# Pacing table lookups by shares of a tile, with all gates transposed on TensorE, in a fused attention and lookup-FFN block

## The chip, the cores and the metric

The kernel runs on one core of a Trainium2 chip, in float32. A core has five engines with instruction queues of their own: TensorE (PE in the profile; its weight loads are PEld), VectorE (DVE), ScalarE (ACT), GpSimd (POOL) and SyncE (SP, which here only issues transfers). Each engine works through its queue strictly in order, and waits for the others by semaphores. Transfers are issued from SP's, ScalarE's or GpSimd's queue and run on 16 DMA engines. The metric is the device time of one execution in microseconds.

## What is computed

Input x has 8 sequences of 1024 tokens of 512 features. Per sequence:

```python
xn = layernorm(x)
q = xn @ Wq; gate = softmax(xn @ Wg)            # three gates for each token
for i in range(3):
    k, v = xn @ Wk[i], xn @ Wv[i]
    w = sigmoid(decay[i]) ** max(t - s - 1, 0) * (s after t)
    blended += gate[..., i:i+1] * (((q @ k.T) * w) @ v)
s = blended @ Wo * out_scale
W = lut[idx]                                     # 16 values; gate, up and down matrices, 1376 x 512 each
h = silu(xn @ Wgate.T) * (xn @ Wup.T)
out = x + s * silu(h @ Wdown.T)
```

## The kernel before, in words

There are two phases. Phase 1, to about 597 us, does the normalization, the projections, the attention recurrence and the building of the lookup weights, and writes its results to DRAM. Phase 2 does the two FFN products from there, with a seven-product scheme whose sums are made beforehand. The diff touches phase 1 alone.

Phase 1 is written as coroutines (Python generators) that one loop interleaves; every `yield` ends a portion of work. After tracing, `keep_order` fixes each engine's order to the order in which the instructions were written. So what decides when an instruction gets its turn is where its coroutine was resumed.

The loop of `phase_1` runs over sequences b (one more round than there are sequences) and in each over 8 steps k. A step resumes, in three thirds:

- `newer`, `project` of sequence b. It loads 128-token chunks of x, makes their statistics, normalizes them, transposes them on TensorE (`pt`, copied by ScalarE to `xnT`), and multiplies with the value and gate weights (`values`, tile `pv`). From step 4 on it also runs `features` for half 1 of the tokens, which makes queries and keys by seven products out of sums `t1` to `t4` (tile `ts`; `t1` on L505) that VectorE makes, and `softmax`, which makes the gates.
- `ending`, the last part of `project` of sequence b-1: `features` and `softmax` for half 0. It runs in steps 0 to 3.
- `older`, `chunks` of sequence b-1: the recurrence over chunks c = 7 to 0. TensorE transposes the keys (`pk`), makes scores (`psc`), adds to the state (`pu`) and makes the output (`po`, first with the factor `qb`, then with `pr`). VectorE makes `pr` out of `psc` (L652), and `ga`, the gated queries of the next chunk (L627); GpSimd makes `qb` out of `ga` (L631). ScalarE copies `po` to `bl` (L675), which is one buffer for all sequences and goes to DRAM at the end of each (L689).
- `weights`, the building of the lookup weights, through `build_some`, three times in a step.

The lookup of a tile (`look_up`, 128 partitions x 1024 indices; some tiles are narrower) is 19 VectorE instructions: three mask bits (L218), one on the index's lowest bit (L221), eight leaves (L225), seven selections (L242). Then GpSimd makes sums of the tile: four of 256 elements a partition (L272 to L276, or L322 to L326), and after every second tile four of 896 elements (L290 to L300, or L339 to L346). A looked-up tile lies in one of two `wgu` buffers. SP loads the indices of a tile while the tile before it is looked up.

`build_some(n)` resumes the building n times. The counts in the loop are 1, 0 and 0 or 1, 1 and 2 for b = 0, and for b = 1 to 7 they go (1, 1, 4), (1, 2, 5), (1, 2, 4), (1, 2, 3). A sum on GpSimd counts as one resumption like an instruction on VectorE, and some resumptions do nothing (three behind a pair of tiles, eight behind a pair of the down matrix).

The gates of half a sequence (`g`, 128 tokens x 12) must lie in DRAM as 12 rows of 128, so that they can be loaded into all partitions (`ga`, L473). `write` stores g's 1536 words one by one from SP's queue (L458). For (b, half) = (0, 1) alone, `turn` transposes g on TensorE (`pg`, L463), lets ScalarE copy it (`gs`, L465) and stores 12 rows from ScalarE's queue (L466). `pg` takes one of the three rotating PSUM buffers of tag `c`, which `pt`, `pv`, `pk`, `psc` and `po` share. `defer(n, ...)` holds an issue back for n calls of `tick()`, of which a step has three; the load of `ga` is deferred by 6.

Of the kernel before, what the change touches and what calls it, by code (L numbers as in the profile page):

```python
# [9 lines left out]
F32 = mybir.dt.float32  # L10
# [4 lines left out]
ALU = mybir.AluOpType  # L15
AX = mybir.AxisListType

P = 128
# [30 lines left out]
def recurrent_block(ctx: ExitStack, tc, x, wq, wk, wv, wo, wg, decay_logits, out_scale, lut, gidx, uidx, didx, out):  # L49
# [52 lines left out]
    bl_d = [dram.tile([P, T], F32, name=f"bld{b}", tag=f"bld{b}") for b in range(B)]  # L102
# [31 lines left out]
    def defer(parts, issue):  # L134
        later.append([parts, issue])
# [77 lines left out]
    def look_up(build, dst, iv, rows, n):  # L213

        bits = [build.tile([P, n], U8, name=f"bit{j}", tag=f"bit{j}") for j in (1, 2, 3)]
        low = iv.bitcast(U8).rearrange("p (n four) -> p n four", four=4)[:, :, 0]
        for j in (1, 2, 3):
            nc.vector.tensor_scalar(bits[j - 1][:rows, :n], low, 1 << j, None, ALU.bitwise_and)  # L218
            yield

        nc.vector.tensor_scalar(iv, iv, 31, 31, ALU.logical_shift_left, ALU.arith_shift_right)  # L221
        yield

        def leaf(o, k):
            nc.vector.tensor_scalar(  # L225
                o.bitcast(I32),
                iv,
                lut_x[:rows, k, :],
                lut_i[:rows, k, 0:1],
                ALU.bitwise_and,  # L230
                ALU.bitwise_xor,
            )

        def tree(o, level, k):
            if level == 0:
                leaf(o, k)
                yield
                return
            t = build.tile([P, n], F32, name=f"leaf{level}", tag=f"leaf{level}")
            yield from tree(o, level - 1, k)  # L240
            yield from tree(t[:rows, :n], level - 1, k + (1 << (level - 1)))
            nc.vector.copy_predicated(o, bits[level - 1][:rows, :n], t[:rows, :n])  # L242
            yield

        yield from tree(dst, 3, 0)

    def ffn_weights(build, pool, pair_pool):
# [8 lines left out]
        upper = []  # L256

        def gate_up(o):
            s, m = OCH[o]
# [42 lines left out]
            for _ in range(3):  # L302
                yield

        def down_tail():
            s, m = OCH[-1]
            idx = build.tile([P, NB], I32, name="idx", tag="idx", bufs=2)
            nc.sync.dma_start(out=idx[:m, :V], in_=didx[s : s + m, :])
            yield
            wf = pool.tile([P, 2 * NB], F32, name="wgu", tag="wgu", bufs=2)  # L310
            yield from look_up(build, wf[:m, :V], idx[:m, :V], m, V)
            defer(2, lambda: nc.sync.dma_start(out=wdt_d, in_=wf[:m, :V]))

        def down(rows, e, ends):
            idx = build.tile([P, NB], I32, name="idx", tag="idx", bufs=2)
            for a, row in enumerate(rows):
                nc.sync.dma_start(out=idx[:, ts(a, V)], in_=didx[ts(row, P), :])
            yield
            t = pool.tile([P, 2 * NB], F32, name="wgu", tag="wgu", bufs=2)
# [3 lines left out]
            nc.gpsimd.tensor_tensor(t2, b22, t1, ALU.subtract)  # L323
            yield
            nc.gpsimd.tensor_tensor(b12, b22, b12, ALU.subtract)
# [13 lines left out]
            nc.gpsimd.tensor_tensor(pair[:, :, 0], b12, b11, ALU.subtract)  # L339
            yield  # L340
            nc.gpsimd.tensor_tensor(b12, b22, b12, ALU.subtract)
            defer(2, lambda: nc.sync.dma_start(out=to[:, :, 0:2, :], in_=up))
            yield
            nc.gpsimd.tensor_tensor(pair[:, :, 1], b22, pair[:, :, 0], ALU.subtract)
            yield
            nc.gpsimd.tensor_tensor(pair[:, :, 2], b21, pair[:, :, 1], ALU.subtract)  # L346
            defer(4, lambda: nc.sync.dma_start(out=to[:, :, 4:7, :], in_=pair))
            for _ in range(8):
                yield
# [4 lines left out]
        yield  # L354
        for job, following in zip(jobs, jobs[1:] + [iter(())]):
# [21 lines left out]
    def project(b, pools, sides, kept):  # L377
# [61 lines left out]
        def softmax(hf):  # L439
# [15 lines left out]

            def write():
                with nc.allow_non_contiguous_dma(reason="1536 words"):
                    nc.sync.dma_start(out=there.rearrange("k p -> p k"), in_=g.rearrange("p c i -> p (c i)"))  # L458

            def turn():  # L460

                pg = p_c.tile([n * NI, P], F32, name=f"pg{b}_{hf}", tag="c")
                nc.tensor.transpose(pg, g.rearrange("p c i -> p (c i)"), ident)  # L463
# [9 lines left out]
            defer(6, lambda: nc.sync.dma_start(out=ga, in_=there.partition_broadcast(P)))  # L473

        def features(hf):
# [4 lines left out]

            qk[hf] = att.tile([P, NI + 1, U], F32, name=f"qk{b}_{hf}", tag=f"qk{hf}", bufs=1)
            c11, c12, c21, c22 = (qk[hf][:, 2 * j : 2 * j + 2, ts(c, H)] for j in (0, 1) for c in (0, 1))
            ts_ = tp.tile([P, 4, 2, H], F32, name=f"ts{b}_{hf}", tag=f"ts{hf}")
            b11, b12, b21, b22 = (xnT[:, 2 * v : 2 * v + 2, ts(2 * hf + c, H)] for v in (0, 1) for c in (0, 1))
            t1, t2, t3, t4 = (ts_[:, k] for k in range(4))
            a11, a12, s3, a22 = (wqk_sb[:, 2 * v : 2 * v + 2, ts(j, 2 * D)] for j in (0, 1) for v in (0, 1))
            s1, s2, s4 = (wqs[:, k] for k in range(3))
# [16 lines left out]
            there = xs_d[b][:, :, ts(hf, H)]  # L504
            nc.vector.tensor_tensor(t1, b12, b11, ALU.subtract)  # L505
            yield
            product(pa, 1, True)
# [55 lines left out]
        for k in range(NC):  # L563
# [25 lines left out]
            if k >= NC // 2:  # L589
                next(of_half, None)  # L590
            yield
        of_half = features(0)
        for k in range(NC // 2):
            yield
            if k == 0:
                next(of_half)
            next(of_half)
            half = softmax(0) if k == 0 else iter(())
            next(half, None)
            yield  # L600
            next(half, None)
            next(of_half, None)
            yield
# [10 lines left out]
    def chunks(b, pools, kept):  # L614
# [20 lines left out]
        for c in reversed(range(NC)):  # L635
# [52 lines left out]
            yield  # L688
        (nc.scalar if at_end else nc.sync).dma_start(out=bl_d[b], in_=bl)  # L689

    def phase_1():
        nonlocal small, p_a, p_c, p_r
        with (
# [21 lines left out]

            def build_some(n):
                for _ in range(n):
                    next(weights, None)

# [11 lines left out]
            for b in range(B + 1):  # L731
                following = project(b + 1, pools, sides, kept) if b + 1 < B else iter(())
                older = chunks(b - 1, (chk, blp), kept) if b else iter(())
                for k in range(NC):


                    if b == 0:
                        steps = (k > 0, k >= NC // 2, 2 * (k >= NC // 2))
                    elif b < B:
                        steps = ((1, 1, 4), (1, 2, 5), (1, 2, 4), (1, 2, 3))[k % 4]  # L740
                    else:
                        steps = (1, 0, 0)
                    tick()
# [12 lines left out]
                    next(newer, None)  # L756
                    build_some(steps[1])
                    next(older, None)
                    build_some(steps[2])
                    if k < NC // 2:  # L760
# [680 lines left out]
```

## Time and profile before

| | |
|---|---|
| three runs | 2112.64, 2113.19, 2113.54 us (median 2113.19) |
| the profiled execution | 2114.02 us, of which the span of the instructions is 2111.9 |
| granted TensorE clock, mean | 0.999 |
| 0 to 600 us: PE, DVE, ACT, POOL busy | 582.8, 511.2, 374.2, 302.0 us |
| 600 to 2111 us: PE, DVE, ACT, POOL busy | 1505.8, 933.0, 569.5, 738.4 us |
| lookups on VectorE (L218, L221, L225, L242) | 51, 17, 136 and 119 instructions |
| `gTd<-g`, the stores of gates by words | 15, of 6 KB, 14.7 us from issue to landing |
| `bld<-bl` | 7 from SP's queue, of 512 KB, 3.0 us |

In the profile an engine's idle time is put down to what ended it. The end of a matmul is modelled, so that a shown wait of TensorE is somewhat shorter than what the distance between two starts tells. A float32 matmul of the program shows as two in the profile, a transpose as one.

### The profile page before, as it was taken

What the parts mean: (1) busy time and instruction counts of PE and PEld (TensorE: products, weight loads), DVE (VectorE), ACT (ScalarE), POOL (GpSimd) and SP (SyncE); (2) the same over time, 40 slices, a digit from 0 to 9 for tenths busy, and PEclk for the clock granted to TensorE, in tenths of its full rate; (3) what the DMA queues carried; (4) which work ended last, traced back from release to release, by engine and by line L of the source; (5) the groups of instructions that cost most, each with busy time, mean ns of one, the idle gap of its engine ahead of it and who ended that gap; (6) DMA issues with size and microseconds to landing.
All of it is one profiled execution on the core that took longest, in us unless ns stands there. A gap on an engine that the chain in (4) does not pass through costs nothing.

```text
span 2111.9 us, 32189 instructions
## 1 busy us (share of the span) xinstructions
PE 2088.6 (99%) x11691; PEld 1752.9 (83%) x11691; DVE 1444.2 (68%) x2214; ACT 943.6 (45%) x2116; POOL 1040.4 (49%) x1050
## 2 busy tenths in 40 slices
PE   9999999999999999999999999999999999999999
PEld 7877878888878888887878888887978888797877
DVE  8889897889735675575567556656755665675567
ACT  4766666676434424423441442344144324423531
POOL 4554564364445447516543751655275255527432
PEclk9999999999999999999999999999999999999999
DMA  8765779657864744464454446345544634464442
GB/s 217 146 180 165 188 176 199 161 153 138 157 204 150 256 155 159 162 223 142 157 196 174 157 147 245 136 155 173 197 160 151 248 123 153 160 223 147 150 155 108
DMA packets 184635, 361.51 MB, mean 171 GB/s; under 512 B 50927, under 2 KB 122238, under 8 KB 184478
## 3 DMA queue, kind: packets, MB, share of 16 engines
q1 hardware_dynamic: 169894, 335.20, 52.7%
q0 software_dynamic: 4480, 14.68, 1.7%
q10 hardware_dynamic: 10104, 9.58, 1.5%
q8 instruction: 93, 1.52, 0.3%
q14 instruction: 64, 0.52, 0.1%
HBM read 282.87 MB, written 76.55 MB: 170 GB/s over the span
## 4 chain that ended last, share of the span: by engine, by line
PE 76%; DVE 3%; DMA 1%; issue 0%; ACT 0%; SPq 0%; DVEq 0%; ACTq 0%
PE s L885 33%; PE sE L885 6%; PE s12d L1139 5%; PE s21d L1139 5%; PE s11d L1139 5%; PE fs L833 3%; PE pd L1252 3%; PE ps L1259 3%; PE sEd L1139 2%; PE fsE L833 1%; PE pv L434 1%; PE s11d L1150 1%; PE s21d L1150 1%; PE s12d L1150 1%; PE sEd L1150 1%; PE po L674 1%
## 5 line engine op out<-in xcount | busy, mean ns | idle before, releaser
L885 PE MATMUL s<-xs,wq 128*128 128x256 f32 x3264 | 731.2, 379 | 0.0
L885 PEld LDWEIGHTS s<-xs,wq 128*128 128x128 f32 x3264 | 619.5, 190 | 95.9 <-issue 8.4
L908 DVE TENSOR_TENSOR s<-s,e 128x512 f32<-128x512 f32 x136 | 95.1, 699 | 204.4 <-ACT s L907 204.3
L1223 POOL TENSOR_TENSOR cu<-cu 128x256 f32<-128x256 f32 x32 | 35.1, 1097 | 306.4 <-DVE cl L1222 306.4
L434 PE MATMUL pv<-wvg_sb,xnT 128*128 128x387 f32 x512 | 177.6, 488 | 0.0
L816 POOL TENSOR_TENSOR xs<-xs 128x256 f32<-128x256 f32 x224 | 170.9, 789 | 8.1 <-PE fs L833 3.5
L912 DVE TENSOR_TENSOR sE<-s,e 128x512 f32<-128x512 f32 x136 | 95.0, 698 | 104.6 <-PE s L885 104.6
L976 POOL TENSOR_TENSOR u<-u,e 128x512 f32<-128x512 f32 x64 | 79.9, 1270 | 148.8 <-DVE u L972 130.3
L903 ACT COPY e<-sE 128x512 f32<-128x512 f32 x136 | 79.6, 585 | 138.8 <-PE sE L885 138.5
L885 PE MATMUL sE<-xs,wq 128*128 128x256 f32 x544 | 139.6, 379 | 0.0
L434 PEld LDWEIGHTS pv<-wvg_sb,xnT 128*128 128x128 f32 x512 | 94.4, 191 | 53.9
L980 POOL TENSOR_TENSOR h<-h,u 128x512 f32<-128x512 f32 x64 | 80.1, 1272 | 112.9 <-DVE u L987 100.3
L896 ACT COPY s<-s 128x512 f32<-128x512 f32 x136 | 77.5, 570 | 109.0 <-PE s L885 106.7
L413 POOL TENSOR_SCALAR rstd<-rstd 128x1 f32<-128x1 f32 x56 | 28.8, 515 | 192.3 <-ACT junk L412 186.4
L907 ACT COPY s<-s 128x512 f32<-128x512 f32 x136 | 77.5, 570 | 98.1 <-PE s L885 98.1
L1139 PE MATMUL s12d<-wdd,z 128*128 128x128 f32 x896 | 118.5, 275 | 0.6 <-ACT s12d L1161 0.6
L885 PEld LDWEIGHTS sE<-xs,wq 128*128 128x128 f32 x544 | 103.4, 190 | 14.1
L1139 PEld LDWEIGHTS s12d<-wdd,z 128*128 128x128 f32 x896 | 109.0, 192 | 0.8 <-ACT s12d L1161 0.8
L631 POOL TENSOR_TENSOR qb<-ga,q_tab 128x384 f32<-128x384 f32 x56 | 79.0, 1410 | 55.0 <-DVE ga L627 49.0
L225 DVE TENSOR_SCALAR leaf<-idx,lut_x,lut_sb 128x1024 int32<-128x1024 int32 (+2 forms) x119 | 96.5, 832 | 0.0
L242 DVE COPY_PREDICATED leaf<-bit,leaf 128x1024 f32<-128x1024 uint8 (+2 forms) x68 | 94.2, 1385 | 1.5
L1263 POOL TENSOR_TENSOR gx<-gx,cu 128x512 f32<-128x512 f32 x32 | 40.7, 1277 | 82.0 <-DVE cu L1261 64.5
(263 smaller groups left out, 4534.2 us busy)
## 6 DMA issues: line engine op xcount, KB each, us to landing
wq<-quadd SPq DMA_DIRECT2D x112, 896.0 KB, 4.5
wdd<-wdd SPq DMA_DIRECT2D x56, 896.0 KB, 4.6
xs<-xsd SPq DMA_DIRECT2D x56, 512.0 KB, 6.1
wq<-quadd SPq DMA_DIRECT2D x48, 448.0 KB, 4.1
x<-in_x SPq DMA_DIRECT2D x64, 256.0 KB, 4.7
xsd<-ts SPq DMA_DIRECT2D x16, 1024.0 KB, 14.9
gx<-in_x SPq DMA_DIRECT2D x64, 256.0 KB, 5.3
out<-gx POOLq DMA_DIRECT2D x56, 256.0 KB, 2.3
```

What stands on the lines that cost most here:

```text
L225: nc.vector.tensor_scalar(o.bitcast(I32), iv, lut_x[:rows, k, :], lut_i[:rows, k, 0:1], ALU.bitwise_and, ALU.bitwise_xor,)
L242: nc.vector.copy_predicated(o, bits[level - 1][:rows, :n], t[:rows, :n])
L434: nc.tensor.matmul(pv, lhsT=xnT[:, v, ts(c, P)], rhs=wvg_sb[:, v, :], start=(v == 0), stop=(v == NV - 1))
L816: nc.gpsimd.tensor_tensor(o, x1, x2, ALU.subtract)
L833: nc.tensor.matmul(ps, lhsT=w[:, 2 * W_OF[k] + n, :m], rhs=xs[:, X_OF[k], 2 * n : 2 * n + 2, :], start=start and n == 0, stop=stop and n == 1,
L885: nc.tensor.matmul(self.t[n][:, ts(a, H)], lhsT=self.w[:, a, (0, 1, 6, 3, 4, 5, 2)[i - 1], :], rhs=self.xs[:, X_OF[self.ks[a]], D_OF[i], : ...
L908: nc.vector.tensor_tensor(self.t[1], self.t[1], self.e, ALU.add)
L912: nc.vector.tensor_tensor(self.t[3], self.t[2], self.e, ALU.add)
L976: nc.gpsimd.tensor_tensor(o[:, n], o[:, n], other[:, n], ALU.add)
L980: nc.gpsimd.tensor_tensor(of_h(half, n), of_h(half, n), two(other[:, n]), ALU.mult)
L1139: nc.tensor.matmul(self.t[n][:, ts(a, P)], lhsT=self.lhs[i][:, e, ts(a, P)], rhs=self.w[:, e, D_OF[i], :], start=start and a == 0 and e == ...
L1150: nc.tensor.matmul(self.t[n][:, ts(a, P)], lhsT=self.left[:, ts(2 * (n // 2) + a, P)], rhs=wd_left[:, D_OF[self.k], ts(n % 2, P)], start=F ...
```

## The change

The building is paced by shares of a tile: each `yield` in it now yields a number, and `build_some` goes on while less has been done than is due. A sum counts 0.07 and a wide sum 0.14, the empty resumptions are gone, and narrow tiles count by their width. `features` makes `t1` first, and its first portion is resumed one third of a step earlier, at the end of steps 3 and 7. The store of `bl` always goes through ScalarE's queue. All gates are turned by TensorE, a third of a step later than the words were stored (3 ticks for 2).

```diff
     def look_up(build, dst, iv, rows, n):
+        part = n / NB
...
             nc.vector.tensor_scalar(bits[j - 1][:rows, :n], low, 1 << j, None, ALU.bitwise_and)
-            yield
+            yield 0.04 * part
         nc.vector.tensor_scalar(iv, iv, 31, 31, ALU.logical_shift_left, ALU.arith_shift_right)
-        yield
+        yield 0.04 * part
...
                 leaf(o, k)
-                yield
+                yield 0.045 * part
...
             nc.vector.copy_predicated(o, bits[level - 1][:rows, :n], t[:rows, :n])
-            yield
+            yield 0.07 * part
...
+        SUM, WIDE_SUM = 0.07, 0.14
...
             nc.sync.dma_start(out=iv[:, 6:8, :], in_=us[:, 2:4, :])
-            yield
+            yield 0.0
...
             nc.gpsimd.tensor_tensor(s2, s1, a11, ALU.subtract)
-            yield
+            yield SUM
...
             nc.gpsimd.tensor_tensor(pair[:, :, 0], b21, b22, ALU.add)
-            yield
+            yield WIDE_SUM
...
             defer(4, lambda: nc.sync.dma_start(out=to[:, :, 4:7, :], in_=pair))
-            for _ in range(3):
-                yield
...
             ga = gates[-1]
-            if (b, hf) == (0, 1):
-                defer(3, turn)
-            else:
-                defer(2, write)
+            defer(3, turn)
             defer(6, lambda: nc.sync.dma_start(out=ga, in_=there.partition_broadcast(P)))
...
             t1, t2, t3, t4 = (ts_[:, k] for k in range(4))
+            nc.vector.tensor_tensor(t1, b12, b11, ALU.subtract)
+            yield
+            qk[hf] = att.tile([P, NI + 1, U], F32, name=f"qk{b}_{hf}", tag=f"qk{hf}", bufs=1)
...
             there = xs_d[b][:, :, ts(hf, H)]
-            nc.vector.tensor_tensor(t1, b12, b11, ALU.subtract)
-            yield
             product(pa, 1, True)
...
                     values(c + 1)
                     lag = 0
-                of_half = features(1)
-                next(of_half)
             if k >= NC // 2:
                 next(of_half)
...
                 next(of_half, None)
-            yield
-        of_half = features(0)
+            if k in (NC // 2 - 1, NC - 1):
+                of_half = features(k // (NC // 2) ^ 1)
+                next(of_half)
+            yield
         for k in range(NC // 2):
             yield
-            if k == 0:
-                next(of_half)
             next(of_half)
...
-        (nc.scalar if at_end else nc.sync).dma_start(out=bl_d[b], in_=bl)
+        nc.scalar.dma_start(out=bl_d[b], in_=bl)
...
-            def build_some(n):
-                for _ in range(n):
-                    next(weights, None)
+            due = 0.0
+
+            def build_some(part):
+                nonlocal due
+                due += part
+                while due > 0.0:
+                    due -= next(weights, 1.0)
...
                     if b == 0:
-                        steps = (k > 0, k >= NC // 2, 2 * (k >= NC // 2))
+                        parts = (0.05 * (k > 0), 0.05 * (k >= NC // 2), 0.1 * (k >= NC // 2))
                     elif b < B:
-                        steps = ((1, 1, 4), (1, 2, 5), (1, 2, 4), (1, 2, 3))[k % 4]
+                        parts = ((0.05, 0.05, 0.18), (0.05, 0.1, 0.26), (0.05, 0.1, 0.25), (0.05, 0.1, 0.2))[k % 4]
                     else:
-                        steps = (1, 0, 0)
+                        parts = (0.05, 0.0, 0.0)
...
-                    build_some(steps[0])
+                    build_some(parts[0])
```

More of the change, by code (lines that the diff above doesn't have):

```diff
@@ L290, in gate_up @@
             nc.gpsimd.tensor_tensor(pair[:, :, 0], b21, b22, ALU.add)
-            yield
+            yield WIDE_SUM
             nc.gpsimd.tensor_tensor(pair[:, :, 1], pair[:, :, 0], b11, ALU.subtract)
-            yield
+            yield WIDE_SUM
             if o >= 4 * NQ:
                 for _ in range(4):
-                    yield
+                    yield SUM
             nc.gpsimd.tensor_tensor(b21, b11, b21, ALU.subtract)
             defer(3, lambda: nc.sync.dma_start(out=to[:, :, 2:4, :], in_=low))
-            yield
+            yield WIDE_SUM
             nc.gpsimd.tensor_tensor(pair[:, :, 2], b12, pair[:, :, 1], ALU.subtract)
             defer(4, lambda: nc.sync.dma_start(out=to[:, :, 4:7, :], in_=pair))
-            for _ in range(3):
-                yield
         def down_tail():
@@ L308, in down_tail @@
             nc.sync.dma_start(out=idx[:m, :V], in_=didx[s : s + m, :])
-            yield
+            yield 0.0
             wf = pool.tile([P, 2 * NB], F32, name="wgu", tag="wgu", bufs=2)
@@ L317, in down @@
                 nc.sync.dma_start(out=idx[:, ts(a, V)], in_=didx[ts(row, P), :])
-            yield
+            yield 0.0
             t = pool.tile([P, 2 * NB], F32, name="wgu", tag="wgu", bufs=2)
@@ L323, in down @@
             nc.gpsimd.tensor_tensor(t2, b22, t1, ALU.subtract)
-            yield
+            yield SUM
             nc.gpsimd.tensor_tensor(b12, b22, b12, ALU.subtract)
@@ L339, in down @@
             nc.gpsimd.tensor_tensor(pair[:, :, 0], b12, b11, ALU.subtract)
-            yield
+            yield WIDE_SUM
             nc.gpsimd.tensor_tensor(b12, b22, b12, ALU.subtract)
             defer(2, lambda: nc.sync.dma_start(out=to[:, :, 0:2, :], in_=up))
-            yield
+            yield WIDE_SUM
             nc.gpsimd.tensor_tensor(pair[:, :, 1], b22, pair[:, :, 0], ALU.subtract)
-            yield
+            yield WIDE_SUM
             nc.gpsimd.tensor_tensor(pair[:, :, 2], b21, pair[:, :, 1], ALU.subtract)
             defer(4, lambda: nc.sync.dma_start(out=to[:, :, 4:7, :], in_=pair))
-            for _ in range(8):
-                yield
         jobs = [gate_up(o) for o in range(NO)] + [down_tail()]
@@ L353, in ffn_weights @@
         next(jobs[0])
-        yield
+        yield 0.0
         for job, following in zip(jobs, jobs[1:] + [iter(())]):
@@ L454, in softmax @@
             there = gT_d[b][ts(hf, n * NI), :]
-            def write():
-                with nc.allow_non_contiguous_dma(reason="1536 words"):
-                    nc.sync.dma_start(out=there.rearrange("k p -> p k"), in_=g.rearrange("p c i -> p (c i)"))
             def turn():
@@ L468, in softmax @@
             ga = gates[-1]
-            if (b, hf) == (0, 1):
-                defer(3, turn)
-            else:
-                defer(2, write)
+            defer(3, turn)
             defer(6, lambda: nc.sync.dma_start(out=ga, in_=there.partition_broadcast(P)))
         def features(hf):
-            qk[hf] = att.tile([P, NI + 1, U], F32, name=f"qk{b}_{hf}", tag=f"qk{hf}", bufs=1)
-            c11, c12, c21, c22 = (qk[hf][:, 2 * j : 2 * j + 2, ts(c, H)] for j in (0, 1) for c in (0, 1))
             ts_ = tp.tile([P, 4, 2, H], F32, name=f"ts{b}_{hf}", tag=f"ts{hf}")
@@ L485, in features @@
             t1, t2, t3, t4 = (ts_[:, k] for k in range(4))
+            nc.vector.tensor_tensor(t1, b12, b11, ALU.subtract)
+            yield
+            qk[hf] = att.tile([P, NI + 1, U], F32, name=f"qk{b}_{hf}", tag=f"qk{hf}", bufs=1)
+            c11, c12, c21, c22 = (qk[hf][:, 2 * j : 2 * j + 2, ts(c, H)] for j in (0, 1) for c in (0, 1))
             a11, a12, s3, a22 = (wqk_sb[:, 2 * v : 2 * v + 2, ts(j, 2 * D)] for j in (0, 1) for v in (0, 1))
@@ L504, in features @@
             there = xs_d[b][:, :, ts(hf, H)]
-            nc.vector.tensor_tensor(t1, b12, b11, ALU.subtract)
-            yield
             product(pa, 1, True)
@@ L756, in phase_1 @@
                     next(newer, None)
-                    build_some(steps[1])
+                    build_some(parts[1])
                     next(older, None)
-                    build_some(steps[2])
+                    build_some(parts[2])
                     if k < NC // 2:
```

## The prediction

> **What bounds the kernel now.** I read the page first, then TensorE's waits, then the timelines around the longest of them. The diff touches phase 1 alone (to 597 us), and TensorE is busy all through:
>
> ```profile
> PE 2088.6 (99%) x11691; PEld 1752.9 (83%) x11691; DVE 1444.2 (68%) x2214; ACT 943.6 (45%) x2116; POOL 1040.4 (49%) x1050
> ```
>
> So the change can only win what TensorE stands idle, and whatever it adds to TensorE's queue counts in full. The waits:
>
> ```profile
> PE po L674 <- DVE pr L652: 9.1, 9, 1.8
> PE pe L495 <- DVE ts L505: 2.1, 3, 0.9
> PE psc L650 <- ACT bl L675: 1.8, 1, 1.8
> PE fs L833 <- DMA wq<-quadd: 1.6, 1, 1.6
> ...
> PE po L674 <- POOL qb L631: 0.4, 1, 0.4
> ```
>
> (us in all, times, longest.) As ends are modelled, I took the distance between matmul starts instead, less the usual distance of that shape: 16.3 us for the waits on VectorE and GpSimd and the small ones beside them, 3.7 us for the one on `bl`. Why `pr` is late shows VectorE's timeline:
>
> ```profile
> 275.10 3.16 DVE L218 TENSOR_SCALAR bit<-idx 128x1024 uint8<-128x1024 uint8 x2
> ...
> 278.67 2.60 DVE L514 TENSOR_TENSOR ts<-xnT 128x512 f32<-128x512 f32 x1
> 281.19 2.61 DVE L218 TENSOR_SCALAR bit<-idx 128x1024 uint8<-128x1024 uint8 x1
> 283.72 1.48 DVE L520 TENSOR_TENSOR ts<-xnT,ts 128x512 f32<-128x512 f32 x1
> ```
>
> Bits and sums usually take 0.68 (medians of L218 and L514). Here they take up to 2.6, while GpSimd works without a pause from 268.6 to 286.8 (eight sums, then `rstd` and `qb`). VectorE then runs behind for several chunks.
>
> **Pacing.** A step of TensorE, `psc` to `psc`, is 9.5 us (8.8 into chunk 6, 9.2 into chunk 0, 7.1 into chunk 7). I went through the start of every `pr` and the end of its `psc`: TensorE stalls once `pr` starts more than 4.05 us after its `psc` (2.4 for chunks 4 and 0, which have less work between). I then added up VectorE's work between one `pr` and the next in the written order, at 0.95 for a bit, 1.05 for L221 (near their means in the trace), 0.73 for a leaf and 1.33 for a selection (distances of their starts), and medians for the rest. Against the distances from `pr` to `pr` in the trace this is mostly right within 0.5 us, except beside GpSimd's sums, where it falls short by 2 to 6. The start of it, sequence.chunk with us before and after:
>
> ```
> 0.3  3.8  2.9   0.2  9.4  8.3   0.1  9.4 10.0   0.0  8.6  7.2   1.7  7.4  9.6   1.6  9.9  8.6
> 1.5  6.5  8.6   1.4  5.7  1.8   1.3  7.1  8.2   1.2  9.9  8.4   1.1  9.7 10.0   1.0  8.7  8.5
> ```
>
> No lookup is added or removed. But GpSimd's eight sums, 4 x 1.0 + 4 x 2.2 = 13 us, now spread over three steps where they were written into one or two, and VectorE gets its empty step in one piece (1.4). Now the backlog is carried on: what one stretch has over TensorE's step is added, what it has less is taken off, down to nothing. Bits and L221 count 0.68 where GpSimd rests (1.2 us less a tile), and 4.5 us is added where they meet its sums. After the change 0.2 gives 8.3 - 1.2 + 4.5 - 9.5 = 2.1 us late, 0.1 2.6, 0.0 0.6, 1.7 0.6 + 9.6 - 1.2 - 7.1 = 1.9, 1.6 1.7, 1.5 0.8, 1.4 nothing; the empty step wipes it out, and so on. The peak is 3.2, at 2.6. Before, `pr` was 3.0 to 6.1 late at its thirteen stalls. `t1`, `ga` and `pr` share the queue, so `t1`'s stalls are in this too. `t1` itself comes sooner by one or two lookups, but `ga` of chunk 7 now stands behind it, and its `psc` comes 0.7 us before the product of `t1`: at 1.7, 0.6 + 0.55 + 5.3 (4.1 if its bits meet no sum) + 0.55 us pass from `psc` of 0.0 to `ga`'s end, where TensorE takes 6.2, a stall of 0 to 0.8. By these sums 1 to 2 us of stall are left. I take 3.5, as VectorE's spare time is small. Ends for what is left: 0 and 9. **-12.8** (-16.3 to -7.3). `qb`'s waits, behind GpSimd's sums, are in it.
>
> **The store of `bl`.** SP's queue is late, as it waits for 106 us in all on words of gates and 33 on L297:
>
> ```profile
> SPq L473 <- DMA gTd<-g: 106.0, 12, 11.8
> 355.65 0.27 ACT L675 COPY bl<-po 128x128 f32<-128x128 f32 x1 [4.84 <-DMA bld<-bl]
> ```
>
> The store of sequence 3 is issued at 349.1 us, and ScalarE stands 4.84 us on it. Issued by ScalarE behind its last copy and landing in 3.0, it is done before the next copy to `bl` some 8 us on. In the same place the granted clock was 0.5 from 356.8 for 3.4 us, right behind TensorE's 1.85 us of idleness; eight matmuls took 0.21 more each, 1.7 us of the 3.7. **-3.7**; if the dip comes elsewhere all the same, -2.0.
>
> [...]
>
> **The gates.** 15 stores by words go, and with them SP's waits; what SP issues behind them comes sooner, which nothing on TensorE waits for but the last: `ga` at 584.7 costs VectorE 1.28 and TensorE 0.36. **-0.4**, to -1.2 with the loads of phase 2, whose first matmul waits 1.6. Those I count no gain for: SP's waits show that x for phase 2 is held by the last `ts` store (1.5) and by the product that ends at 582.4 (0.4), which do not move against TensorE. Added: 15 transposes. The one there is:
>
> ```profile
> 28.89 0.27 PE L463 MATMUL pg<-ident,g 128*12 128x128 f32 x1
> 29.00 2.77 PE L434 MATMUL pv<-wvg_sb,xnT 128*128 128x387 f32 x8
> ```
>
> 0.27 long, but the next matmul starts 0.11 behind it: 15 x 0.11 = **+1.65**. [...] ScalarE gets 15 x (0.25 copy + 0.60 issue, and about 0.65 between), 22 us in 570 where it idles a third; `pc`, `qk` and `v` copies queue behind. `pg` also waits for g of VectorE, and shifts the three PSUM buffers by one. In half 0 it follows `pk` of chunk 6, 6.4 us behind `psc` of chunk 7, and g takes 4.4 us from `pr` on (5.5 at most), so `pr` may be 2 late; I expect 0 to 0.3 at a few places. `wdld`, on ScalarE's queue a little earlier, may hold it once. Together **+0.8** (0 to +3).
>
> **The start.** Here shares bring a stall. Two bits are now written in step 1, before the normalization of chunk 4, and they wait for the first indices:
>
> ```profile
> 12.19 0.55 DVE L419 TENSOR_SCALAR x<-x,mean,rstd 128x512 f32<-128x512 f32 x1 [0.32 <-POOL rstd L407]
> 14.92 0.69 DVE L218 TENSOR_SCALAR bit<-idx 128x1024 uint8<-128x1024 uint8 x1 [1.12 <-DMA idx<-in_uidx]
> 14.57 0.60 PE L427 MATMUL pt<-ident,x 128*128 128x128 f32 x4
> ```
>
> The normalization then starts at 14.92 + 2 x 0.62 = 16.2 and ends at 16.75 instead of 12.74; chunk 4's transpose, at 14.57 before, starts at 16.8: **+2.25** (1.5 to 2.75). Nothing later gives it back, as TensorE has no idle time in the first 70 us. SP also loads the second indices ahead of the keys' weights (512 KB, some 2 us): these arrived at 18.5 and are first used at 20.66, now 22.9, so the stall covers it; without it they would cost up to 0.3. A clock dip behind a gap this long, at half a chance of 1.7: **+0.85** (0 to 1.7).
>
> **Sum**, against the profiled execution's 2114.02 (its span 2111.9 and 2.1 around it): -12.8 - 3.7 - 0.4 + 1.65 + 0.8 + 2.25 + 0.85 = -11.35, 2102.7. The median of the runs is 0.83 lower: 2101.8, say **2102**. All ends together, taken from the median, are 2095.0 (2113.19 - 16.3 - 3.7 - 1.2 + 1.65 + 1.5) and 2113.0 (2113.19 - 7.3 - 2.0 + 1.65 + 3 + 2.75 + 1.7).
>
> **Rivals**, beside it (0.52, 2095 to 2105):
> - *Half the stalls stay*: the lookups are 16.25 tiles of 19.05 us at the prices above, 44 for each of seven sequences, and VectorE has 19 more of its own and 2 to 6 a pair beside GpSimd: up to 69 of TensorE's 72.6 (5 x 9.5 + 8.8 + 9.2 + 7.1), so a slip lasts. For it: `pr` was 3.0 to 6.1 late. Against it: the empty step now comes whole after each pair. Stalls left 8 instead of 3.5: 2106. Chance 0.24.
> - *The stalls only move*, to `ga` behind `t1` and to chunk 0, and 14 stay: 2101.8 + 10.5 = 2112, no change to tell. For it: the same work on VectorE, and two limits, at chunks 0 and 4, of only 2.4. Chance 0.14.
> - *The turn holds TensorE* (slower): `pg` in TensorE's queue waits for VectorE's g, and for a PSUM buffer that ScalarE frees. Before, a late g delayed a transfer only. If `pr` of chunk 7 stays 2.5 to 3 late as at 125 us, each turn costs about 0.7 to 1.3 more; it decides from 1.05 a turn: 15 x 1.05 = 15.8, 2118. Against it: half 1's turns have 9.4 us for 5. Chance 0.10.
>
> Faster by over 0.2% (under 2109; about what a measurement of this kernel tells from no change): 0.52 + 0.24 = 0.76. Within 0.2%: 0.14. Slower: 0.10. The range takes in the first two cases and most of the third: 2095 to 2113.
>
> **What would show it.** TensorE's waits: `po` on `pr` under 3 us in all, no `psc` on `bl`, one new `pt` on `x` of about 2 us near 15 us. GpSimd's L290 to L300 in three steps, SP without waits on `gTd`, 16 `pg`. Wrong if waits of `psc` on `ga` or of `pg` on g sum to over 3 us, or if bits beside GpSimd stretch to over 6 us a pair again.

## The result, and the profile after

The changed kernel takes 2144.87 us (median of 4 runs, 2142.92 to 2145.5) against 2112.91 beside it: a ratio of 1.0148, interval 1.0133 to 1.0164, 32 us slower. The prediction was 2102. In the profiled execution the span is 2141.1 instead of 2111.9. Phase 2's first matmul starts at 627.9 us instead of 598.7, so the loss lies in phase 1. In the new file `pr` is L645, `po` L667, `ga` L620, the bits L222, `pv` L437, `pg` L461.

The page's busy times first, then TensorE's waits (us in all, times, longest):

```profile
PE 2098.6 (98%) x11706; PEld 1755.0 (82%) x11706; DVE 1439.9 (67%) x2214; ACT 946.6 (44%) x2131; POOL 1031.8 (48%) x1050
```

```profile
PE pv L437 <- DVE pr L645: 22.8, 10, 4.6
PE po L667 <- DVE pr L645: 3.9, 3, 2.2
PE pt L430 <- DVE x L422: 2.5, 2, 2.0
PE psc L643 <- ACT ks L639: 1.6, 1, 1.6
...
PE pg L461 <- DVE g L455: 0.9, 1, 0.9
```

The old wait of `po` on `pr` has shrunk from 9.1 to 3.9, the one on `bl` is gone, and a new one stands on top: `pv` waits for `pr`. But `pv` multiplies x with weights and reads nothing of `pr`. The timelines of TensorE and VectorE show how it stands:

```profile
95.27 0.83 PE L643 MATMUL psc<-ga,qk 128*128 128x128 f32 x6
95.93 0.27 PE L461 MATMUL pg<-ident,g 128*12 128x128 f32 x1
100.50 3.89 PE L437 MATMUL pv<-wvg_sb,xnT 128*128 128x387 f32 x6 [4.30 <-DVE pr L645]
```

```profile
92.36 1.65 DVE L455 TENSOR_TENSOR g<-g,sm 128x12 f32<-128x12 f32 x1
...
94.53 1.48 DVE L225 TENSOR_SCALAR idx<-idx 128x1024 int32<-128x1024 int32 x1
95.94 2.60 DVE L515 TENSOR_TENSOR ts<-xnT,ts 128x512 f32<-128x512 f32 x1
98.46 0.80 DVE L229 TENSOR_SCALAR wgu<-idx,lut_x,lut_sb 128x1024 int32<-128x1024 int32 x1
99.18 0.80 DVE L229 TENSOR_SCALAR leaf<-idx,lut_x,lut_sb 128x1024 int32<-128x1024 int32 x1
99.91 0.54 DVE L645 TENSOR_TENSOR pr<-psc,w_tab 128x384 f32<-128x384 f32 x1
```

`g` is ready at 94.0, in time for `pg`. `pv`, right behind `pg`, must wait until `pr` has read `psc`, at 100.45. The reason stands in the built program, in the PSUM bank that each tile of tag `c` has got (here for chunk 2 of sequence 0):

```
before:  pt 6  pk 5  psc 4        pv 6  po 4
after:   pt 5  pk 6  psc 4  pg 5  pv 4  po 6
```

Before, `pv` got the bank of `pt`, and `po` that of `psc`. Now `pg` takes the bank of `pt`, and `pv` gets that of `psc`: in all seven sequences with such a turn. `pr` used to be needed by `po`, some 4 us later; now it is needed at once. TensorE at the same place before:

```profile
92.50 0.83 PE L650 MATMUL psc<-ga,qk 128*128 128x128 f32 x6
93.16 2.77 PE L434 MATMUL pv<-wvg_sb,xnT 128*128 128x387 f32 x8
...
100.16 0.91 PE L674 MATMUL po<-qb,R 128*128 128x128 f32 x6 [1.83 <-DVE pr L652]
```

The granted clock follows in the windows (us, then busy time of PE, PEld, DVE, ACT, POOL, then PEclk, DMA share, GB/s):

```profile
80.00:100.00 20.00, 16.20 (x100) 13.65 (x98) 14.91 (x18) 15.55 (x44) 18.88 (x16) 1.00 0.24 82
100.00:120.00 20.00, 19.50 (x100) 15.67 (x101) 15.36 (x17) 9.50 (x25) 4.08 (x5) 0.91 0.56 193
400.00:420.00 20.00, 15.37 (x71) 11.65 (x70) 18.81 (x35) 9.44 (x27) 7.18 (x10) 0.83 0.52 174
```

At five of the seven waits the clock drops to 0.5 (from 100.5, 179.0, 257.5, 411.1 and 568.1 us), and the matmuls of `pv` take 0.32 us more each, 1.5 to 2.7 us a time.

As in the prediction, I take the distances between matmul starts less the usual one of the shape, here for phase 1 (us; the columns hold single excesses over 0.3 us, the last one all of them, small ones too):

```
                        pv behind  slower  po on  psc on  pe on  psc on  pg, pv in  start  all
                        pg         pv      pr,qb  ga      ts     bl      half 0
before                  -          -       11.1   -       2.6    2.0     -          -      27.4
after                   22.6       8.8     4.4    4.3     -      -       4.0        2.2    54.2
place alone (e16)       -          -       6.8    8.4     -      -       -          2.3    25.9
words again (e1)        -          -       12.1   8.4     -      -       -          1.9    32.6
best of the shares (e14) -         -       9.1    1.0     -      -       -          -      19.9
the same, words (e15)   -          -       16.7   1.0     -      -       -          -      29.9
bl and t1 only (e12)    -          -       10.6   2.0     -      -       -          -      20.5
```

With 15 x 0.11 for the transposes, the change's sum is 54.2 - 27.4 + 1.65 = 28.5, and the spans differ by 29.2.

### The profile page after: what moved, and what is told of

Its sections match the earlier page's. It is cut to its first block, busy times and chain, and to the rows that moved or that the text cites. A ratio compares the mean times of both kernels' runs of the same rounds, so it can differ in the third digit from the quotient of the medians.

```text
span 2141.1 us, 32224 instructions
## 1 busy us (share of the span) xinstructions
PE 2098.6 (98%) x11706; PEld 1755.0 (82%) x11706; DVE 1439.9 (67%) x2214; ACT 946.6 (44%) x2131; POOL 1031.8 (48%) x1050
## 4 chain that ended last, share of the span: by engine, by line
PE 84%; DVE 9%; ACT 1%; issue 1%; POOL 0%; DMA 0%; ACTq 0%; SPq 0%; DVEq 0%; POOLq 0%
PE s L882 33%; PE sE L882 5%; PE s12d L1136 5%; PE s21d L1136 5%; PE s11d L1136 5%; PE pv L437 4%; PE fs L830 3%; PE pd L1249 3%; PE ps L1256 3%; PE po L667 2%; PE sEd L1136 2%; DVE leaf L229 2%; PE pc L492 2%; DVE leaf L246 1%; PE fsE L830 1%; PE s11d L1147 1%
## 5 line engine op out<-in xcount | busy, mean ns | idle before, releaser
L437 PE MATMUL pv<-wvg_sb,xnT 128*128 128x387 f32 x512 | 187.8, 511 | 22.9 <-DVE pr L645 22.8
L437 PEld LDWEIGHTS pv<-wvg_sb,xnT 128*128 128x128 f32 x512 | 97.8, 198 | 84.7 <-DVE pr L645 26.7
L229 DVE TENSOR_SCALAR leaf<-idx,lut_x,lut_sb 128x1024 int32<-128x1024 int32 (+2 forms) x119 | 107.9, 933 | 0.0
L246 DVE COPY_PREDICATED leaf<-bit,leaf 128x1024 f32<-128x1024 uint8 (+2 forms) x68 | 89.3, 1313 | 1.5
```

The lines of the kernel that those rows point to most:

```text
L229: nc.vector.tensor_scalar(o.bitcast(I32), iv, lut_x[:rows, k, :], lut_i[:rows, k, 0:1], ALU.bitwise_and, ALU.bitwise_xor,)
L437: nc.tensor.matmul(pv, lhsT=xnT[:, v, ts(c, P)], rhs=wvg_sb[:, v, :], start=(v == 0), stop=(v == NV - 1))
```

## The experiments

Times are medians in us. Each ratio is against the kernel before, measured beside the run (medians 2112.5 to 2114.6), with its 95% interval. Where no other file is named, the edit is against the changed kernel.

### The turns and the place of pg

**e1_words**

```diff
-            defer(3, turn)
+            if (b, hf) == (0, 1):
+                defer(3, turn)
+            else:
+                defer(2, write)
```

> The changed kernel with the gates stored by words again, as before (only half 1 of sequence 0 is turned by TensorE). The lookups by shares, t1 sooner and bl stored by ScalarE stay. Theory (the turns cost the time: pg takes a PSUM buffer, pv gets the one that psc left and must wait until pr has emptied it): off 2144.9 come the seven waits of pv (22.6 us by distances of starts), the slower matmuls behind them (about 9.5), the waits of psc, pg and pv on ScalarE and VectorE in half 0 (7 to 8) and 15 x 0.11 of transposes, so about 2104 (2099 to 2109), and pr at chunk 2 is as late as in the changed kernel (3 to 5 us after psc in most sequences) without any stall of pv. Rival (the shares make pr late, and TensorE would wait for it anyway, at po): 2125 or more.

2123.21, ratio 1.0044 (1.0030 to 1.0059): neither the theory's 2104 nor the rival's 2125. `pv` does not wait behind `pg`, so the turns do cost most of the loss, but 9 us against before stay: `po` waits 12.1 us for `pr` again, and `psc` 8.4 at chunk 7, which it did not before. Two of `po`'s waits, of 4 us each, stand behind a wait of VectorE for a store.

**e2_turns_only**

```diff
# before.py
-            if (b, hf) == (0, 1):
-                defer(3, turn)
-            else:
-                defer(2, write)
+            defer(3, turn)
```

> The kernel before with one edit: all gates are turned by TensorE and stored as rows. Theory: pv of chunk 2 waits for pr as in the changed kernel. In the trace of before pr of chunk 2 ends 6.96, 5.03, 3.88, 4.05, 0.87, 0.87 and 1.83 us after the start of its last psc matmul, where pv then started 0.11 behind it; less 0.17 each, that is 22 us of waits, plus some 8 for slower matmuls behind the long ones, 7 in half 0, 1.65 for the transposes, less some 6 of the old waits of po that now are paid at pv: about 2146 (2135 to 2155). Rival (the shares are the cause, the turns cost their 1.65 and ScalarE's time): 2113 to 2120.

2143.11, ratio 1.0140 (1.0125 to 1.0155). As the theory says: `pv` waits 22.1 us for `pr` by the profile. The turns cost 29 us in the kernel before too, without any shares.

**e4_half0**

```diff
-            defer(3, turn)
+            if hf == 0 or b == 0:
+                defer(3, turn)
+            else:
+                defer(2, write)
```

> The changed kernel, with half 1 of sequences 1 to 7 stored by words and half 0 of all turned by TensorE. Theory: the seven waits in half 1 and the slower matmuls go (32 us) with 7 x 0.11 of transposes: about 2112 (2107 to 2117); against the kernel without turns 7 to 9 us remain for half 0, as pv of chunk 6 gets the buffer of psc and psc that of pt. Rival (half 0's small waits only take the place of others): the same as without turns, 2104. Rival (the shares are the cause): 2130 or more.

2123.25, ratio 1.0048 (1.0033 to 1.0063): the same as e1_words, as the rival "the same as without turns" has it, though both lie far above its 2104. The waits that half 0 adds (`pg` 1.6, `pv` 1.9) are given back at `po`, which waits 7.3 instead of 12.1, as one of its two waits behind a store is gone. By this pair half 1 costs all of the 21.7 us between e1_words and the changed kernel; e16_place_alone below says that half 0 isn't always free.

**e3_later_pg**

```diff
-            defer(3, turn)
+            defer(3 if b == 0 or hf == 0 else 5, turn)
```

> The changed kernel, with the turns of half 1 two ticks later (sequence 0 excepted): pg is then issued behind pk of chunk 1, and in the built program pv of chunks 2 and 1 gets a buffer that pt or pk left, none that pr must empty. The same transposes, copies and stores. Theory: the seven waits of pv (22.6) and the slower matmuls behind them (9.5) go, half 0 stays: about 2113 (2108 to 2119). Rival (a turn costs what it costs wherever it stands, through ScalarE's copies and issues or a late g): 2135 or more.

2138.34, ratio 1.0117 (1.0102 to 1.0132). The expectation missed, because I had looked at one sequence's banks only. `pv` of chunk 1 gets the bank of `pk` in three of the seven sequences and that of `psc` in four. Both cost: the waits are 3.5, 3.5 and 1.0 us behind `ks`, ScalarE's copies of `pk`, which stand behind its normalization, and 3.1, 1.9, 4.6 and 3.5 behind `pr`. So the run does not show that a turn costs by itself; it shows that at this place, too, `pg` leaves `pv` a bank whose reader is late.

**e5_pg_at_po**: `pg` just ahead of `po`, which waits for `pr` in any case.

```diff
+    turns = []
...
-            defer(3, turn)
+            if b and hf:
+                defer(3, lambda: turns.append(turn))
+            else:
+                defer(3, turn)
...
+            while turns:
+                turns.pop()()
             po = p_c.tile([P, P], F32, name=f"po{b}_{c}", tag="c")
```

> The changed kernel with the same turns, stores and loads, but in half 1 of sequences 1 to 7 pg stands just ahead of po of chunk 2 instead of ahead of pv. In the built program pv then gets the buffer of pt in all seven, pg that of psc, which po took before and which pr must empty for po in any case. Theory (the place of pg among the buffers is what costs, not the turning): the seven waits of pv and the slower matmuls behind them (32 us of 2144.9) go, and so do the two waits of VectorE for stores on SP's queue that cost 4.1 and 4.0 us in the run with words, as no words are written: 2115 (2110 to 2121). Rival (a turn in half 1 costs some 3 us wherever pg stands, through ScalarE's copies and issues, a late g or a late ga): 2130 or more.

2119.47, ratio 1.0022 (1.0013 to 1.0032): 25 us faster than the changed kernel, with the same transposes, copies, stores and loads.

**e10_before_pg_at_po**: the same edit in e2_turns_only.

> The kernel before with all gates turned by TensorE, as in e2_turns_only, but with pg of half 1 of sequences 1 to 7 just ahead of po instead of ahead of pv; half 0 as there. Theory (place among the buffers): of e2_turns_only's 2143.1 the waits of pv behind pg in half 1 (18.6 us over 0.4 us each, by distances of starts) and the slower matmuls behind them (about 7) go: 2118 (2113 to 2124). Rival (turning itself, with its copies and stores on ScalarE, costs the 29): 2132 or more.

2123.07, ratio 1.0050 (1.0036 to 1.0064): 20 of the 29 us are gone. The rest is mostly half 0, where `pg` waits 8.7 us for `g` and ScalarE (3.2 of them while ScalarE itself waits for the store of `bl`), and `pv` 5.4 for `pr`.

**e16_place_alone**: e5_pg_at_po with half 0's turns ahead of `po` as well.

```diff
-            if b and hf:
+            if b or not hf:
                 defer(3, lambda: turns.append(turn))
```

> The changed kernel with nothing altered but the place of pg, now ahead of po in both halves (half 1 of sequence 0 excepted). Theory: e5_pg_at_po's 2119.5 less the waits that half 0's turns make there (pg on g and on ScalarE 1.6 us, pv on pr 1.8): 2116 (2113 to 2119). Rival (half 0's turns cost nothing, as in the run with half 0 alone): 2119 or more.

2114.44, ratio 1.0006 (0.9997 to 1.0015): no different from before, 30.4 us faster than the changed kernel, with nothing else altered. Against e5_pg_at_po (1.0013 to 1.0032) half 0's place is worth some 3 us by the ratios, 5 by the medians. The changed kernel and this one are the plainest pair of the study. TensorE at the place shown above, in e16_place_alone:

```profile
94.74 0.83 PE L647 MATMUL psc<-ga,qk 128*128 128x128 f32 x6
95.40 2.77 PE L438 MATMUL pv<-wvg_sb,xnT 128*128 128x387 f32 x8
98.02 1.89 PE L496 MATMUL pa<-xnT,wqk_sb 128*128 128x256 f32 x8
99.74 0.83 PE L657 MATMUL pu<-v,ks 128*128 128x128 f32 x6
100.41 0.27 PE L462 MATMUL pg<-ident,g 128*12 128x128 f32 x1
100.52 0.83 PE L673 MATMUL po<-qb,R 128*128 128x128 f32 x6
```

`pr` is as late as it was. From the start of the last matmul of `psc` to the end of `pr`, at chunk 2 of sequences 0 to 6:

```
after            4.63  3.70  2.87  1.43  4.96  2.54  3.64
e16_place_alone  4.65  3.72  2.89  1.42  4.97  2.37  3.60
```

There it stalls nothing, as `pv`, `pa` and `pu` run meanwhile; in the changed kernel nearly all of it was a stall. The clock in e16_place_alone is 0.999.

### The lookups by shares

**e8_shares_only**: the kernel before with the `yield` and `build_some` parts of the diff only.

> The kernel before with the lookups by shares alone (t1, the gates and bl as before). By the prediction's step: 12.8 us of stalls go, the start costs 2.25 to 3.1: about 2104. Theory now: the shares only move the stalls, and without the empty steps a lookup's first leaf comes before the store that still reads its tile has landed, behind the words on SP's queue (in the run with words VectorE waited 2.2 and 6.6 us there and TensorE 4.1 and 4.0 behind it); with the start and the stall of bl: 2118 to 2125.

2127.41, ratio 1.0059 (1.0044 to 1.0074): worse than even the new theory. All excesses of distances add up to 40.6 us (27.4 before): `po` 13.6, of which 9.5 in two places behind stores, `psc` 5.1 at chunk 7, `pe` 4.5, the start 2.9.

**e6_old_t1**: e5_pg_at_po with `t1` and `features` resumed where they were before.

> The run e5_pg_at_po with t1 back where it was before the change (written with the product that reads it, behind ga). Theory A (t1 ahead of ga delays ga of chunk 7, and psc waits for it: 7.6 us in five places in the run with words, against 2.5 us that pe waited for t1's followers before): 5 us faster than e5_pg_at_po, near 2110. Theory B (what delays ga are the three bits and the shift that shares put ahead of it, 4 to 5 us; t1 is only 0.6 us of it): within 2 us of e5_pg_at_po.

2121.88, ratio 1.0037 (1.0022 to 1.0051), 2.4 us slower than e5_pg_at_po, which the intervals don't quite separate; the traces do. `psc`'s stalls at chunk 7 fall by 3.4 (to 5.1), and `pe`'s on `ts` appear (4.5). So `t1` sooner pays a little at most, and Theory B is nearer: the bits ahead of `ga` delay it more than `t1`. VectorE and then TensorE between chunk 0 and chunk 7, in e5_pg_at_po:

```profile
117.21 0.55 DVE L649 TENSOR_TENSOR pr<-psc,w_tab 128x384 f32<-128x384 f32 x1
117.67 3.28 DVE L223 TENSOR_SCALAR bit<-idx 128x1024 uint8<-128x1024 uint8 x3
120.98 1.10 DVE L226 TENSOR_SCALAR idx<-idx 128x1024 int32<-128x1024 int32 x1
122.12 0.82 DVE L230 TENSOR_SCALAR wgu<-idx,lut_x,lut_sb 128x1024 int32<-128x1024 int32 x1
122.85 0.69 DVE L483 TENSOR_TENSOR ts<-xnT 128x512 f32<-128x512 f32 x1
123.45 0.55 DVE L624 TENSOR_TENSOR ga<-ga,qk 128x384 f32<-128x384 f32 x1
```

```profile
119.35 1.89 PE L496 MATMUL pa<-xnT,wqk_sb 128*128 128x256 f32 x8
124.11 0.91 PE L647 MATMUL psc<-ga,qk 128*128 128x128 f32 x6 [2.86 <-ACT pb L507]
```

The profile names ScalarE's `pb` for `psc`, but `ga` ends at 124.00 and `psc` starts 0.1 later. It is so at all five of these stalls, so what they wait for is `ga`.

**e11_start_c7**

```diff
# e5_pg_at_po
-                        parts = (0.05 * (k > 0), 0.05 * (k >= NC // 2), 0.1 * (k >= NC // 2))
+                        parts = (0.05 * (k > 1), 0.05 * (k >= NC // 2), 0.1 * (k >= NC // 2))
...
+                        if k == 0:
+                            parts = (0.15, 0.05, 0.18)
+                        if k == NC - 1:
+                            parts = (0.05, 0.1, 0.1)
```

> e5_pg_at_po with two shares moved: none at step 1 of sequence 0 (so that the normalization of chunk 4 is not behind bits that wait for indices), and 0.1 of the third share of chunk 0's step goes to the first share of chunk 7's step, behind ga. Theory: the start's 2.0 us go, and of the 8.4 us in which psc of chunk 7 waits for ga most: 2111 (2107 to 2115). Rival (VectorE has no time to spare, so what is not written ahead of ga makes pr of chunk 7 late): within 3 us of e5_pg_at_po, 2117 or more.

2118.73, ratio 1.0034 (1.0022 to 1.0046): the total did not move, as the rival has it, but its parts did. `psc`'s stalls fall from 8.4 to 1.3, as the theory said. But `g` in half 0 is late now, behind what was moved, and `pg` waits 9.1 us for it; the rival had expected the delay at `pr`. The start got worse (3.5): the load of the indices had moved along with the bits.

**e13_all_po**: e11_start_c7 with `if b or not hf:` as in e16_place_alone.

> e11_start_c7 with half 0's turns, too, just ahead of po. Theory: the waits of pg in half 0 (1.6 us in e5_pg_at_po) and of pv on pr there (1.8) go: 2 to 4 us faster than e11_start_c7, near 2108. Rival (half 0's turns cost nothing where they stand, as the run with half 0 alone equalled the run with words): the same as e11_start_c7.

2108.74, ratio 0.9983 (0.9974 to 0.9992): 10 us faster than e11_start_c7. With half 0's `pg` ahead of `po`, a late `g` stalls nothing.

**e14_start**

```diff
# e13_all_po
-                        parts = (0.05 * (k > 1), 0.05 * (k >= NC // 2), 0.1 * (k >= NC // 2))
+                        parts = (0.04 * (k > 1), 0.05 * (k >= NC // 2), 0.1 * (k >= NC // 2))
+                        if k == 1:
+                            next(weights)
```

> e13_all_po with the load of the first indices at step 1 of sequence 0 and no bit before step 2, where before had its first. Theory: the start's stall (2.9 us in e13_all_po) goes, nothing else moves: 2105.8 (2103 to 2108). Rival (the bits wait for the indices wherever they stand, and the normalization behind them): 2108 or more.

2107.25, ratio 0.9970 (0.9959 to 0.9982). The start's stall is gone, but `po` waits 9.1 us for `pr` instead of 6.7. The median is 1.5 us below e13_all_po's, which these intervals don't separate.

**e15_start_words**: e14_start with the gates stored as in e1_words.

> e14_start with the gates stored by words, as before (half 1 of sequence 0 alone is turned). Theory (words hold SP's queue, a store of a looked-up tile behind them lands late, and without the empty steps VectorE's first leaf of the next lookup but one waits for it, and TensorE's po behind that): 5 to 10 us slower than e14_start, 2111 to 2116, with VectorE's wgu waiting for quadd in its waits. Rival (those waits came from shares placed otherwise; turned or not is worth no more than the 1.65 of the transposes): 2102 to 2107.

2118.02, ratio 1.0019 (1.0010 to 1.0029): 10.8 us slower than e14_start, a little more than the theory's 5 to 10. VectorE's waits in phase 1, and the first of the two places:

```profile
DVE wgu L230 <- DMA quadd<-wgu: 12.2, 2, 8.1
```

```profile
289.13 0.68 DVE L226 TENSOR_SCALAR idx<-idx 128x1024 int32<-128x1024 int32 x1
293.85 0.81 DVE L230 TENSOR_SCALAR wgu<-idx,lut_x,lut_sb 128x1024 int32<-128x1024 int32 x1 [4.04 <-DMA quadd<-wgu]
```

```profile
295.34 0.83 PE L661 MATMUL pu<-v,ks 128*128 128x128 f32 x6
301.98 1.41 PE L677 MATMUL po<-qb,R 128*128 128x128 f32 x5 [5.81 <-DVE pr L653]
```

The first leaf of a lookup writes a `wgu` buffer that a store still reads. At both places `po` waits in e14_start too, but shorter: 2.5 and 1.4 us against 6.0 and 7.1, by distances. At the second place SP's queue shows why the store is late. First e15_start_words, then e14_start:

```profile
352.54 2.15 SPq L400 DMA_DIRECT2D x<-in_x  x1
364.30 0.33 SPq L476 DMA_DIRECT2D ga<-gTd  x1
364.73 0.53 SPq L306 DMA_DIRECT2D quadd<-wgu  x1
```

```profile
356.93 0.53 SPq L306 DMA_DIRECT2D quadd<-wgu  x1
```

With words, SP waits on the load of `ga` until the words have landed, and the store of `wgu` behind it goes out 7.8 us later; about 2 of these are the first place's stall. At the first place the store is issued at nearly the same time (285.80 and 286.55), but behind the load of `ga` (768 KB) instead of ahead of it, and VectorE waits 4.04 us instead of 0.67.

### The parts that held

**e7_bl**

```diff
# before.py
-        (nc.scalar if at_end else nc.sync).dma_start(out=bl_d[b], in_=bl)
+        nc.scalar.dma_start(out=bl_d[b], in_=bl)
```

> The kernel before with one edit: bl is stored by ScalarE in every sequence. By the prediction's step: psc's wait on bl (2.0 us) and the slow matmuls behind it (1.7) go, 2110.4. Rival (the wait only makes room that VectorE uses, and its pr is late by as much elsewhere): within 1 us of before.

2111.02, ratio 0.9983 (0.9974 to 0.9992): 3.6 us, as predicted.

**e12_bl_t1**: e7_bl with the part of the diff that moves `t1` and the resumptions of `features`.

> The kernel before with bl stored by ScalarE and t1 sooner, and nothing else of the change. By the prediction's step for t1: pe's waits on t1's followers (2.6 us by distances of starts in e7_bl) go: 2108.5. Rival: ga of chunk 7, now behind t1, is later by 0.6, and psc waits for it: 2111 as without t1.

2107.14, ratio 0.9976 (0.9968 to 0.9985): two small parts of the change, without shares and without turns, beat both kernels. `pe`'s stalls on `ts` (2.6) are gone, 2.0 come at `psc` of chunk 7; `po`'s stay.

## Why the prediction was wrong, point by point

Two steps failed. Of the 43 us between the predicted 2102 and the measured 2144.9, 30.4 come from the place of the turns, where 0.8 was expected for waits, and about 12 from the pacing, which left 15.2 us of stalls instead of 3.5.

- *Pacing, -12.8*: the step failed. In the changed kernel `po` does wait only 4.4 us, but there VectorE catches up while TensorE stands at `pv`. Where it doesn't (e16_place_alone), the stalls on VectorE are 6.8 + 8.4 = 15.2 us, of 13.7 before. That is the rival "the stalls only move", to the places it named (8.4 at `ga` of chunk 7, and `po`'s 6.8 all at chunks 0 and 4, with their limit of 2.4) and in its size (14). One of the prediction's own signs of being wrong came, too: `psc` waits 4.3 us for `ga`.
- *The mis-sized term of the pacing* is how late `pr` is, counted from the end of its `psc`: at 0.2, 0.1 and 0.0 the sums gave 2.1, 2.6 and 0.6 us, and e16_place_alone shows 3.83, 4.49 and 2.84. Most of that arises in the first stretch, beside GpSimd's sums, where `pr` follows `pr` after 13.3 us instead of 11.6: the 4.5 us added there were too few by 1.7. And "a stall of 0 to 0.8" at `ga` rests on it: my 7.0 us from `psc` of 0.0 to the end of `ga` began with the 0.6. With 2.84 it is 9.2, against 6.2 for TensorE: 3.0, and 3.03 was measured there. The highest lateness was 4.84, at 3.4, where only 2.4 is free, and not 3.2 at 2.6. A smaller slip: the sum of the low ends gives 2095.1, not 2095.0, and the one of the high ends leaves out the words' -0.4.
- *Words, "which nothing on TensorE waits for"*: true in the order of before, where VectorE's waits name no store. With the shares of e14_start the first leaf of a lookup meets a store that SP's queue holds back, and the words cost 10.8 us (e15_start_words against e14_start). That it comes too early because the empty resumptions are gone is likely, but no run put them back. The prediction went through SP's queue but didn't ask what of VectorE waits for SP's stores once lookups move.
- *`bl`, -3.7*: right, 3.6 by itself (e7_bl).
- *The turns, +1.65 and +0.8 (0 to 3)*: the price of the transpose held, 0.27 us and a distance of 0.11. The step that failed is "shifts the three PSUM buffers by one". I weighed only whether g would be ready, and it was. I did not ask which tile comes next in the queue and whose bank it gets. That costs 30.4 us (after against e16_place_alone): 22.6 of waits, 8.8 of slower matmuls and 4.0 in half 0, less what VectorE wins meanwhile.
- *The rival "the turn holds TensorE"*, at 0.10, was right in its sign and place. Its mechanism (`pg` waits for a late g, and for a buffer that ScalarE frees) wasn't: `pg` waits 1.7 us in all, and what waits is `pv` behind it, for VectorE. "Half 1's turns have 9.4 us for 5" was an answer about g, and half 1 is where nearly all of it happened.
- *The start, +2.25*: right, 2.18 of stall; e14_start shows that it is the two bits ahead of a normalization. The clock dip behind it (+0.85) didn't come: the granted clock was 1.00 up to 100.5 us. Its half chance was an estimate, from two such gaps in the kernel before, of which one was followed by a dip.
- *The end, -0.4*: right. The wait for the last `ga` (0.36 on TensorE) is gone. `fs` waits 0.65 instead of 1.8, for which I had counted no gain; as it waits 0.78 in e1_words, too, this is not the words' doing.

What can be added up closes: e16_place_alone's stalls less before's are -1.5, the transposes +1.65, and the spans differ by +0.2 (2112.1 and 2111.9); for e14_start -7.5 and +1.65, and the spans differ by -5.8. Not settled is why `po`'s stalls sit at 9 to 11 us in several orders of the lookups (before, e12_bl_t1, e14_start); VectorE's lack of spare time is a plausible reason, and no run took work away from it.

## What to carry to other kernels

A tile added to a rotating pool can cost far more than its own time (here 30 us, for 15 transposes that each push the next matmul back by 0.11): list, from the built program and for every place, which buffer the *next* tiles get and who must empty them, and put the new tile just ahead of a consumer that waits for that very reader anyway. An engine that runs late by a few microseconds is harmless only as long as nothing shortens the distance to who needs it, so note that slack (here 4 us of `pr` to `po`) beside each wait. Before a transfer is called harmless, ask what stands behind it in its queue, and what reuses the buffers of those once the order moves.

## What the runs showed of the hardware

The granted clock fell to 0.5 beside some gaps of TensorE and not beside others, and the length of the gap doesn't settle which. In the changed kernel five gaps ahead of `pv`, of 2.7 to 4.8 us by distances of starts (2.54 to 4.63 by the profile), went with 0.5, and two, of 1.3 and 2.4 (1.10 and 2.21), did not. In the kernel before a gap of 1.85 us by the profile, ended at 355.96, was followed by 0.50 from 356.8 to 360.2, and one of 1.83, ended at 100.16, by 1.00. In e2_turns_only TensorE was busy for 1.60 of the 3.50 us up to 343.5, and the mean clock of the next 4 us was 0.57. In e3_later_pg it stood idle for 3.37 us by the profile, up to 109.06, and the clock stayed at 1.00. Windows of e2_turns_only, then of e3_later_pg (PE busy comes first, the clock third from the end):

```profile
340.00:343.50 3.50, 1.60 (x11) 1.22 (x9) 3.50 (x5) 3.43 (x10) 0.19 (x1) 1.00 0.60 211
343.50:347.50 4.00, 3.82 (x7) 2.14 (x8) 3.96 (x6) 1.54 (x5) 2.16 (x2) 0.57 0.60 210
```

```profile
106.00:109.00 3.00, 0.00 (x0) 0.00 (x0) 2.97 (x5) 2.97 (x9) 0.60 (x1) 1.00 0.64 233
109.00:112.00 3.00, 2.94 (x10) 1.83 (x11) 3.00 (x5) 0.16 (x3) 2.33 (x2) 1.00 0.01 2
112.00:116.00 4.00, 4.00 (x31) 3.82 (x30) 3.93 (x4) 0.75 (x3) 0.70 (x1) 1.00 0.41 125
```

What decides between the two, no run was made to show.

VectorE's sums `ts`, of 128 x 512 float32, take 0.68 us (median of 64 in the changed kernel). Beside a wide sum of GpSimd (95.4 to 98.0 us there) the one at 95.94 took 2.60. That is 1.9 of the 3.8 us by which `pr` started behind its `psc` there.
